# Echelon form for the depthwise filters and seven half groups in parts: an attention and perception kernel on one core

## The chip, the cores and the metric

The kernel runs on one core of a Trainium2 chip. A core has five engines that run their own instruction queues in order: TensorE (PE, matrix products), VectorE (DVE), ScalarE (ACT), GpSimd (POOL) and SyncE (SP, which here only issues DMAs). Products land in PSUM banks of 128 x 512 fp32; everything else lives in SBUF, on 128 partitions. The metric is the device time of the whole kernel in microseconds, from one launch, as the median of several runs.

## The reference

The input is four images of 64 x 64 pixels with 256 channels. Layer 0 is full self attention over the 4096 pixels of an image, with 32 channels for queries and keys. Layer 1 is a depthwise 3x3 convolution with three filters to a channel, two pointwise layers with a GELU between them, and attention over the 3x3 neighbourhood. Cut to what matters here:

```
# layer 0
q, k, v = x @ Wq + bq, x @ Wk + bk, x @ Wv + bv
attn = softmax(q @ k.T)                       # 4096 x 4096 for each image
x = gamma * (attn @ v) + x
# layer 1
perceived = conv(x, w_perc, groups=256) + b_perc      # 768 maps, three filters of 9 taps to a channel
hid = gelu(w_up1 @ perceived + b_up1)                 # 512 x 768
h = x + w_up2 @ hid + b_up2
out = h + local_attention_3x3(h)
```

The pointwise layer after the convolution is linear in the three maps of a channel. So any invertible mix of a channel's three filters, with the inverse mix applied to the three columns of w_up1, gives the same result.

## The kernel before

The 4 x 4096 pixels are cut into 32 slots of 512 queries, eight to an image. A slot goes over the 4096 keys of its image in 16 half groups h = 0 to 15 of 256 keys; the code calls them points and writes h as 2 * G + half. At each point the code issues, in this order:

- the keys and values of the groups ahead, through SP's queue (load_keys, load_values, load_forms);
- high_part of the next half group, where that one is done in parts (ACT);
- energy two half groups ahead: two products into the one buffer e, and exp from e to a tile p on ACT (three buffers);
- jobs[point]: pieces of layer 1 for slots three and five back (hidden_part, update, guide, local_values, scores, local_product), mostly TensorE and VectorE;
- product of this half group: p times the values, added up in the acc banks;
- add_up of the next half group on DVE: the running sum den of the weights p, for the softmax's denominator;
- some steps of the depthwise convolution (perceive) of the slot two back, as many as the list share gives for this point.

An ordinary half group multiplies fp32 p and fp32 values: four products, each of which is two instructions in the trace (acc L402, x8). A half group **in parts** (IN_PARTS, and in_two_sums for the slot) uses fp32r operands instead: p is split into a high part (ACT, tile ph, L388), a low part (DVE, pl, L433) and a combination of both (DVE, gap, tile pg, L434), the values likewise when they are made (vh, vl, vg, L346 to L351, written to memory as packed_f). Three sets of four products (acc L414, x12) then stand for the four fp32 ones. ph, pl and pg have one buffer each. Before, h = 2, 5, 8, 11 and 14 are done so, in 29 of the 32 slots: slots 0, 2 and 31 have none.

perceive makes the six maps of 128 channels (three filters in each half of the channels) of a slot. Tap 0 is an ACT instruction (L587), taps 1 to 8 are one DVE scalar_tensor_tensor each (L591, 128 x 526): 48 in a slot. Twelve cheaper additions (L597) then prepare a fast product of 2 x 2 blocks, whose weights GpSimd makes once from w_up1 (mix_weights, L635). The list mixed holds these 60 steps in order; in the last two slots the lists upper, lower and whole do without the fast product. Slot 31 is the last of the main loop, and a tail outside the loop finishes layer 1.

When the last product of a slot is issued, partial_sums turns and reduces den on DVE, TensorE folds the result (dps, L476), and finish scales acc and adds it to the input (DVE, L479 to L500). In the slots before a new image (7, 15, 23) and in slot 0, the values and keys of blocks to come are projected too (project_v, project_qk). In slot 0, w_perc is loaded at point 8 through GpSimd's queue; w_up1 follows in slot 1 at point 2 and mix_weights in slot 1 at point 8. Watched sums check the result's range, and a slower second version, shifted, would run only if they overflow.

Of the kernel before, what the change touches and what calls it, by code (L numbers as in the profile page):

```python
# [9 lines left out]
F32 = mybir.dt.float32  # L10
F32R = mybir.dt.float32r
AF = mybir.ActivationFunctionType
ALU = mybir.AluOpType
# [3 lines left out]
P = 128  # L17
B, H, W, C = 4, 64, 64, 256
N = H * W
CQK = C // 8  # L20
CH = C // P
HP, WP = H + 2, W + 2
NB = 512
# [5 lines left out]
TAPS = 9  # L29
# [4 lines left out]
MULT = 3  # L34
NPC = MULT * CH
# [4 lines left out]
NG = NT // GRP  # L40
# [8 lines left out]

SPLIT = 4096.0  # L50
BELOW = 1.0 - 2.0**-13
IN_PARTS = (2, 5, 8, 11, 14)


LAG_PERC, LAG_HID, LAG_ATT = 2, 3, 5
# [3 lines left out]
def attention_then_perception_kernel(  # L59
# [19 lines left out]
    nc = tc.nc  # L79

    const = ctx.enter_context(tc.tile_pool(name="const", bufs=1))

    def loaded(src, name, shape=None, queue=None):
        t = const.tile(list(shape or src.shape), F32, tag=name, name=name)
        (queue or nc.sync).dma_start(out=t, in_=src)
        return t
# [10 lines left out]
    def unshifted():  # L97
        fctx = ExitStack()
        pool = fctx.enter_context(tc.tile_pool(name="fast", bufs=1))
# [4 lines left out]
        def tile_of(shape, tag, name, bufs=1):  # L104
            return pool.tile(shape, F32, tag=tag, name=name, bufs=bufs)
# [57 lines left out]
        for r in range(KR):  # L163
            m = near[r * KW : (r + 1) * KW]
            for half in range(2):

                for sign in (1, -1):
                    nc.gpsimd.affine_select(
                        out=m[:, half], in_=m[:, half], compare_op=ALU.is_ge, fill=0.0,
# [13 lines left out]
        for q in range(0, P, SQ):  # L183
            part = fold[q : q + SQ].rearrange("p (j r) -> p j r", r=SQ)
            nc.gpsimd.affine_select(
                out=part, in_=part, compare_op=ALU.not_equal, fill=1.0,
# [29 lines left out]
        def in_parts(s, G, half):  # L216
            return in_two_sums(s) and 2 * G + half in IN_PARTS

# [149 lines left out]
        weights, highs, lows, gaps = {}, {}, {}, {}  # L368
        sums, accs, lsums, lrdens = {}, {}, {}, {}
# [51 lines left out]
        def add_up(s, G, half):  # L421

            p = weights[s, G, half]
            if G == 0 and half == 0:
                sums[s] = tile_of([P, 2, NB], "den", f"den_{s}")
                nc.vector.tensor_copy(sums[s], p)
                return
            den = sums[s]
            nc.vector.tensor_tensor(den, den, p, ALU.add)  # L429
            if in_parts(s, G, half):  # L430
                high = highs[s, G, half]
                low, gap = (tile_of([P, 2, NB], f"p{n}", f"p{n}_{s}_{G}_{half}") for n in "lg")
                nc.vector.tensor_tensor(low.bitcast(F32R), p, high, ALU.subtract)  # L433
                nc.vector.scalar_tensor_tensor(  # L434
                    gap.bitcast(F32R), low, -SPLIT, high, ALU.mult, ALU.add
                )
                lows[s, G, half], gaps[s, G, half] = low, gap
            if G == NG - 1 and half == 1:
                nc.vector.tensor_tensor(den[:, 0, :], den[:, 0, :], den[:, 1, :], ALU.add)
# [163 lines left out]
                    begin(i)  # L603

        def by_turns(outputs, taps, r0, r1):
            return [(i, tap, r0, r1) for tap in taps for i in outputs]

# [18 lines left out]
        lower = by_turns(range(NPC), range(LOW, TAPS), RB - 1, RB)  # L626


        wmix = pool.tile([P, 3, MULT, C], F32, tag="wmix", name="wmix")

        def mix_weights(y11, y12, y21, y22, t1, t2, t4):
            for to, a, b in ((t1, y12, y11), (t2, y22, t1), (t4, y21, t2), (y12, y22, y12)):
                nc.gpsimd.tensor_tensor(to, a, b, ALU.subtract)  # L635

        def blocks_of(w, kin, n):

# [441 lines left out]
        for slot in range(NSLOT):  # L1080
            b, g = divmod(slot, NBLK)
# [20 lines left out]
            if slot == 0:  # L1102
                nxt = [early_jobs[2 * i : 2 * i + 2] for i in range(NG)]
            conv = perceive(slot - LAG_PERC, mixed) if slot >= LAG_PERC else iter(())
            n_mixed = NPC * (TAPS - 1) + MULT * len(MIXED)
            n_steps, stepped = n_mixed, 0


            share = [2, 5, 7, 6, 3, 4, 9, 3, 6, 7, 3, 3, 1, 1, 0, 0]
            if slot == NSLOT - 1:  # L1110

                jobs = [
                    job(hidden_part, k, 0, 0) + job(local_values, k - 1, 1),
                    job(local_denominator, a) + job(hidden_part, k, 0, 1),
                    job(hidden_part, k, 1, 0), job(hidden_part, k, 1, 1) + job(local_product, a, 0),
                    job(update, k, 0), job(update, k, 1) + job(local_product, a, 1),
                    job(guide, k, 0) + job(local_values, k, 0),
                    job(guide, k, 1) + job(local_values, k, 1),  # L1120
                    job(scores, k, 0) + job(hidden_part, k + 1, 0, 0),
                    job(scores, k, 1) + job(local_sum, k - 1) + job(hidden_part, k + 1, 0, 1),
                    job(hidden_part, k + 1, 1, 0) + job(local_total, a + 1)
                    + job(local_reciprocal, a + 1),
                    job(hidden_part, k + 1, 1, 1), job(update, k + 1, 0) + job(border, k),
                    job(local_product, a + 1, 0) + job(update, k + 1, 1),
                    job(local_product, a + 1, 1) + job(local_values, k + 1, 0),
                    job(local_values, k + 1, 1),
                ]
                conv = chain(conv, perceive(slot - 1, upper))  # L1130
                n_steps += NPC * (TAPS - 1)
            for point in range(points):
                G, half = divmod(point, 2)
                after = slot + (G + 1) // NG, (G + 1) % NG
                if half == 0:
                    ahead = slot + (G + 2) // NG, (G + 2) % NG
                    if ahead[0] < NSLOT:
                        load_keys(*ahead)
                    if 0 < ahead[0] < NSLOT:
                        load_values(*ahead)  # L1140
                    if G == NG // 2 and slot + 1 < NSLOT:
                        spread_queries(slot + 1)
                behind = slot + (point + 1) // points, *divmod((point + 1) % points, 2)
                if in_parts(*behind):
                    high_part(*behind)
                if after[0] < NSLOT:
                    energy(*after, half)
                soon = slot + (point + 3) // points, *divmod((point + 3) % points, 2)
                if in_parts(*soon):
                    load_forms(*soon)  # L1150
                for do in jobs[point]:
                    do()
                if slot == NSLOT - 1 and point == NHC + 2 * RING:
                    nc.sync.dma_start(out=wup1[:, :MULT, C:], in_=w_up1[:, :MULT, C:])
                product(slot, G, half)

                if point == 0:
                    add_up(slot, 0, 0)
                if point < points - 1:
                    add_up(slot, *divmod(point + 1, 2))  # L1160
                else:
                    partial_sums(slot)


                if slot < NSLOT - 1:
                    to = sum(share[: point + 1])
                else:
                    to = min(n_steps, -(-(point + 1) * n_steps // (points - 2)))
                    if point < 3:
                        to = min(to, n_mixed // MULT)  # L1170
                while stepped < to:
                    next(conv, None)
                    stepped += 1
                if slot == 0 and point == NG:

                    next(combine)
                    blqk = loaded(b_lqk, "blqk", queue=nc.gpsimd)
                    wperc = loaded(w_perc, "wperc", queue=nc.gpsimd)
                    bperc = loaded(b_perc, "bperc", queue=nc.gpsimd)
                if slot == 1 and point == 2:  # L1180
                    wup1 = loaded(w_up1, "wup1", queue=nc.gpsimd)
                    bup1 = loaded(b_up1, "bup1", queue=nc.gpsimd)
                if slot == 1 and point == NG:
                    wup2 = loaded(w_up2, "wup2", queue=nc.gpsimd)
                    mix_weights(
                        *blocks_of(wup1, MULT, C), *(wmix[:, i] for i in range(3))
                    )
                    bup2 = loaded(b_up2, "bup2", queue=nc.gpsimd)
                    nc.gpsimd.dma_start(out=wlv, in_=w_qkv[:, :, 2 * C :])
                    blv = loaded(b_lv.partition_broadcast(P), "blv", [P, C], queue=nc.gpsimd)  # L1190
                if nxt and half == 1:
                    for do in nxt[G]:
                        do()
                    if slot and G + 2 < NBLK:
                        fetch(slot + 1 + G + 2)
# [470 lines left out]
```

## Time and profile before

| what | value |
|---|---|
| median of 3 runs | 3325.75 us (3325.44 to 3326.32) |
| profiled execution, whole | 3326.11 us |
| its span, first to last instruction | 3323.9 us |
| granted TensorE clock | 0.998 |
| acc L402, direct products | 2936 instructions, 8 to a half group |
| acc L414, products in parts | 3 kinds of 580, 12 to a half group |
| perception taps L591 | 1554 instructions, 1099.6 us |
| sums den L429 | 480 instructions, 602.8 us |
| first copy of a sum, L426 | 32 instructions, 21.9 us |
| DMA | 374.77 MB, 112 GB/s over the span |

In the profile a line names the engine, the operation, the tile it writes and the tiles it reads, then busy time and mean time of one. "Idle before" is how long the engine stood still before such instructions and what ended that. The chain of waits starts from the last instruction and goes back each time to whatever released it, so it lists the work that in fact set the end. Instructions on one engine overlap a little, so the distance from one start to the next is shorter than the duration shown.

### The profile page before, as it was taken

How to read it: one execution, taken by the hardware profiler on the slowest of the kernel's cores; microseconds unless marked ns; L12 is line 12 of the kernel's file. 1: busy time of each engine (PE TensorE's matmuls, PEld its weight loads, DVE VectorE, ACT ScalarE, POOL GpSimd, SP SyncE). 2: the span in 40 equal slices, each digit the busy share in tenths (PEclk: the TensorE clock that was granted, in tenths of full speed). 3: DMA queues.
4: the chain of work that ended last, by engine and by line, in shares of the span. 5: the costliest groups of instructions: out<-in, count | busy, mean ns of one | idle time of the engine just before them, and what ended most of it. 6: DMA issues, size and time to landing. Idle time of an engine off the chain costs nothing.

```text
span 3323.9 us, 34616 instructions
## 1 busy us (share of the span) xinstructions
PE 3298.4 (99%) x11754; PEld 2126.2 (64%) x11754; DVE 2903.3 (87%) x4248; ACT 1276.9 (38%) x1577; POOL 426.4 (13%) x602
## 2 busy tenths in 40 slices
PE   9999999999999999999999999999999999999998
PEld 5556666666666666676666666666666666666655
DVE  3689999878999999987999999997799999999995
ACT  4334433344343333334333433334433434333331
POOL 2200011110111110111001111101110011111021
PEclk9999999999999999999999999999999999999999
DMA  6533333463333333346333333335533333333100
GB/s 189 179 104 105 98 102 103 123 187 124 99 108 108 108 115 97 102 140 196 93 108 98 108 108 108 116 97 159 174 121 92 104 103 108 108 108 108 54 18 27
DMA packets 228743, 374.77 MB, mean 113 GB/s; under 512 B 90080, under 2 KB 91120, under 8 KB 228432
## 3 DMA queue, kind: packets, MB, share of 16 engines
q1 hardware_dynamic: 214928, 339.73, 34.0%
q0 software_dynamic: 5376, 18.26, 1.5%
q10 hardware_dynamic: 8256, 14.49, 1.2%
q8 instruction: 97, 1.59, 0.2%
q14 instruction: 86, 0.70, 0.1%
HBM read 316.51 MB, written 55.05 MB: 112 GB/s over the span
## 4 chain that ended last, share of the span: by engine, by line
PE 96%; DVE 2%; ACT 1%; SPq 0%; issue 0%; DMA 0%; ACTq 0%; DVEq 0%; POOL 0%
PE acc L402 37%; PE acc L414 12%; PE e L378 7%; PE dx L718 6%; PE hid_bc L661 5%; PE hid_gf L661 5%; PE hid_de L661 5%; PE lv L881 3%; PE g L814 3%; PE v L325 3%; PE lo L1015 3%; PE s L922 3%; PE hid_a L661 2%; DVE perc L591 1%; PE qk L259 1%; PE hid L693 1%
## 5 line engine op out<-in xcount | busy, mean ns | idle before, releaser
L402 PE MATMUL acc<-p,v 128*128 128x512 f32 x2936 | 1320.7, 592 | 0.2 <-ACT v L339 0.2
L591 DVE SCALAR_TENSOR_TENSOR perc<-xp,wperc,perc 128x526 f32<-128x526 f32 (+3 forms) x1554 | 1099.6, 773 | 6.8 <-ACT perc L587 6.7
L383 ACT ACTIVATE p<-e 128x1024 f32<-128x1024 f32 x512 | 524.7, 1025 | 1414.0 <-PE e L378 1334.9
L402 PEld LDWEIGHTS acc<-p,v 128*128 128x128 f32 x2936 | 554.0, 190 | 584.1 <-issue 568.5
L429 DVE TENSOR_TENSOR den<-den,p 128x1024 f32<-128x1024 f32 x480 | 602.8, 1256 | 32.2 <-ACT p L383 30.3
L378 PE MATMUL e<-qa,ka 128*128 128x512 f32 x1024 | 450.8, 521 | 5.7 <-ACT p L383 5.7
L947 POOL TENSOR_TENSOR lp<-lp,near 128x396 f32<-128x396 f32 x60 | 79.4, 1323 | 2050.1 <-ACT lp L942 2050.0
L378 PEld LDWEIGHTS e<-qa,ka 128*128 128x128 f32 x1024 | 190.0, 189 | 180.1 <-issue 155.4
L718 PE MATMUL dx<-hid,wup 128*128 128x512 f32 x512 | 229.8, 592 | 0.0
L414 PE MATMUL acc<-ph,v 128*128 128x512 f32 x580 | 184.7, 440 | 0.0
L434 DVE SCALAR_TENSOR_TENSOR pg<-pl,ph 128x1024 fp32r<-128x1024 f32 x145 | 178.1, 1229 | 7.4
L597 DVE TENSOR_TENSOR perc<-perc 128x262 f32<-128x262 f32 x360 | 178.3, 509 | 6.3
L433 DVE TENSOR_TENSOR pl<-p,ph 128x1024 fp32r<-128x1024 f32 x145 | 183.6, 1266 | 0.0
L970 POOL TENSOR_TENSOR lsum<-lsum,lp 128x99 f32<-128x99 f32 (+1 forms) x179 | 170.6, 960 | 11.7
L684 ACT ACTIVATE hid<-hid,bup 128x512 f32<-128x512 f32 x120 | 80.1, 715 | 216.6 <-DVE hid L668 216.6
L718 PEld LDWEIGHTS dx<-hid,wup 128*128 128x128 f32 x512 | 96.6, 189 | 98.3 <-issue 92.9
L414 PE MATMUL acc<-pg,vf 128*128 128x512 f32 x580 | 158.9, 395 | 0.1
L414 PE MATMUL acc<-pl,vf 128*128 128x512 f32 x580 | 157.6, 393 | 0.0
L388 ACT ACTIVATE ph<-p 128x1024 fp32r<-128x1024 f32 x145 | 152.4, 1051 | 0.2
L587 ACT ACTIVATE perc<-xp,bperc,wperc 128x526 f32<-128x526 f32 (+1 forms) x192 | 147.6, 819 | 1.8 <-DVE xp L500 1.8
L414 PEld LDWEIGHTS acc<-pg,vf 128*128 128x128 f32 x580 | 109.0, 188 | 26.5 <-DVE pg L434 0.9
L414 PEld LDWEIGHTS acc<-pl,vf 128*128 128x128 f32 x580 | 109.5, 189 | 25.4 <-DVE pl L433 0.3
(187 smaller groups left out, 3756.7 us busy)
## 6 DMA issues: line engine op xcount, KB each, us to landing
vf<-packed_f SPq DMA_DIRECT2D x145, 512.0 KB, 4.6
ka<-packed SPq DMA_DIRECT2D x1016, 64.0 KB, 1.9
v<-packed_v SPq DMA_DIRECT2D x103, 512.0 KB, 3.7
v<-packed_f SPq DMA_DIRECT2D x145, 256.0 KB, 2.8
v<-packed_v SPq DMA_DIRECT2D x145, 256.0 KB, 2.9
xp<-in_x SPq DMA_DIRECT2D x30, 528.0 KB, 6.7
xc<-in_x SPq DMA_DIRECT2D x56, 256.0 KB, 4.3
out<-lo SPq DMA_DIRECT2D x56, 256.0 KB, 2.1
```

The costliest lines, as they stand in the source:

```text
L378: nc.tensor.matmul(e[:, i, :], lhsT=keys[s, G][:, bass.ts(2 * half + i, P)].bitcast(F32R), rhs=queries[s].bitcast(F32R), start=True, stop= ...
L383: nc.scalar.activation(p, e, AF.Exp)
L402: nc.tensor.matmul(accs[s][c], lhsT=v[:, i, bass.ts(c, P)], rhs=p[:, i, :], start=(first and i == 0), stop=(last and i == 1),)
L414: nc.tensor.matmul(accs[s][to + c], lhsT=w[:, i, bass.ts(c, P)].bitcast(F32R), rhs=x[:, i, :].bitcast(F32R), start=(to > 0 and n == 0 and ...
L429: nc.vector.tensor_tensor(den, den, p, ALU.add)
L433: nc.vector.tensor_tensor(low.bitcast(F32R), p, high, ALU.subtract)
L434: nc.vector.scalar_tensor_tensor(gap.bitcast(F32R), low, -SPLIT, high, ALU.mult, ALU.add)
L591: nc.vector.scalar_tensor_tensor(acc, win, wt, acc, ALU.mult, ALU.add)
L597: nc.vector.tensor_tensor(t[:, to, :], t[:, a, :], t[:, b, :], op)
L661: nc.tensor.matmul(ps[:, n * C : (n + 1) * C], lhsT=w(j), rhs=rows_of(mixes[s, j][:, kind, :]), start=(j == 0), stop=(j == MULT - 1),)
L718: nc.tensor.matmul(ps, lhsT=wup2[:, d, bass.ts(c, P)], rhs=hids[s][:, d, :], start=(d == 0), stop=(d == NHC - 1),)
L970: nc.gpsimd.tensor_tensor(to, to, near_ws[block, half][:, t_, of, :], ALU.add)
```

## The change

The change does five things.

1. IN_PARTS becomes 2, 4, 6, 8, 10, 12, 14: every second half group from 2 on is done in parts in the 29 slots, and the values of those half groups are split when they are made.
2. The three filters of a channel are brought to echelon form in slot 0, at points 5, 6 and 7 (clear_tap, 20 small DVE instructions each): a row exchange by size, then a subtraction that makes one tap zero. Filter 1 loses tap 8, filter 2 loses taps 7 and 8. At points 9 to 14 the matching columns of w_up1 are turned back (turn_weights, four DVE instructions of 128 x 512 each time).
3. by_turns leaves the zero taps out: 42 DVE taps to a slot instead of 48, and 54 steps instead of 60; share is written anew for 54 steps.
4. add_up makes the low part ahead of the sum, and the first sum of a slot is one addition of two tiles, without the copy.
5. w_perc, b_perc and w_up1 are loaded in slot 0 at point 1, and a quarter of the turned w_up1, which mix_weights overwrites, is kept in memory (turned_up) and read back near the end instead of the original.

```diff
-IN_PARTS = (2, 5, 8, 11, 14)
+IN_PARTS = (2, 4, 6, 8, 10, 12, 14)
...
                 sums[s] = tile_of([P, 2, NB], "den", f"den_{s}")
-                nc.vector.tensor_copy(sums[s], p)
                 return
-            den = sums[s]
-            nc.vector.tensor_tensor(den, den, p, ALU.add)
             if in_parts(s, G, half):
                 high = highs[s, G, half]
                 low, gap = (tile_of([P, 2, NB], f"p{n}", f"p{n}_{s}_{G}_{half}") for n in "lg")
                 nc.vector.tensor_tensor(low.bitcast(F32R), p, high, ALU.subtract)
+            den = sums[s]
+            before = weights[s, 0, 0] if (G, half) == (0, 1) else den
+            nc.vector.tensor_tensor(den, before, p, ALU.add)
+            if in_parts(s, G, half):
                 nc.vector.scalar_tensor_tensor(
                     gap.bitcast(F32R), low, -SPLIT, high, ALU.mult, ALU.add
                 )
...
-            return [(i, tap, r0, r1) for tap in taps for i in outputs]
+            return [(i, tap, r0, r1) for tap in taps for i in outputs if tap < TAPS - i % MULT]
...
+        coef = pool.tile([P, MULT, 3, CH], F32, tag="coef", name="coef")
+        ROUNDS = ((1, 2, TAPS - 1), (0, 1, TAPS - 1), (1, 2, TAPS - 2))
+
+        def clear_tap(n):
+            p, q, tap = ROUNDS[n]
+            swap, back, m = (coef[:, n, i, :] for i in range(3))
+            a, b = (scratch[:, i, :] for i in range(2))
...
+            def times(to, k, f, op):
+                v.tensor_tensor(prod, f, k.unsqueeze(2).to_broadcast([P, CH, TAPS + 1]), ALU.mult)
+                v.tensor_tensor(to, to, prod, op)
...
+            times(fp, swap, fq, ALU.add)
+            times(fq, back, fp, ALU.add)
+            times(fp, swap, fq, ALU.add)
...
+            times(fq, m, fp, ALU.subtract)
+            v.tensor_tensor(a, y, b, ALU.mult)
+            times(fq, a, fp, ALU.subtract)
+            v.tensor_tensor(m, m, a, ALU.add)
+
+        def turn_weights(n, half):
+            p, q, _ = ROUNDS[n]
+            up, uq = (wup1[:, half * MULT + i, :] for i in (p, q))
+            swap, back, m = (coef[:, n, i, half : half + 1] for i in range(3))
+            for to, k, of in ((uq, back, up), (up, swap, uq), (uq, back, up), (up, m, uq)):
+                nc.vector.scalar_tensor_tensor(to, of, k, to, ALU.mult, ALU.add)
...
-            share = [2, 5, 7, 6, 3, 4, 9, 3, 6, 7, 3, 3, 1, 1, 0, 0]
+            share = [2, 4, 8, 6, 4, 1, 7, 3, 6, 3, 4, 2, 2, 1, 1, 0]
...
-                    nc.sync.dma_start(out=wup1[:, :MULT, C:], in_=w_up1[:, :MULT, C:])
+                    nc.sync.dma_start(out=wup1[:, :MULT, C:], in_=turned_up)
...
+                if slot == 0 and point == 1:
+                    wb = const.tile([P, CH, MULT, TAPS + 1], F32, tag="wb", name="wb")
+                    nc.gpsimd.dma_start(out=wb[:, :, :, :TAPS], in_=w_perc)
+                    bias = loaded(b_perc, "bperc", queue=nc.gpsimd)
+                    wperc, bperc = wb[:, :, :, :TAPS], wb[:, :, :, TAPS]
+                    wup1 = loaded(w_up1, "wup1", queue=nc.gpsimd)
+                    bup1 = loaded(b_up1, "bup1", queue=nc.gpsimd)
+                if slot == 0 and NG - MULT <= point < NG:
+                    if point == NG - MULT:
+                        scratch = tile_of([P, NB], "rden", "scratch")
...
+                        nc.vector.tensor_copy(bperc, bias)
+                    clear_tap(point - NG + MULT)
+                if slot == 0 and NG < point <= NG + 2 * MULT:
+                    turn_weights(*divmod(point - NG - 1, 2))
                 if slot == 0 and point == NG:
...
-                    wperc = loaded(w_perc, "wperc", queue=nc.gpsimd)
-                    bperc = loaded(b_perc, "bperc", queue=nc.gpsimd)
-                if slot == 1 and point == 2:
-                    wup1 = loaded(w_up1, "wup1", queue=nc.gpsimd)
-                    bup1 = loaded(b_up1, "bup1", queue=nc.gpsimd)
                 if slot == 1 and point == NG:
+                    nc.gpsimd.dma_start(out=turned_up, in_=wup1[:, :MULT, C:])
```

More of the change, by code (lines that the diff above doesn't have):

```diff
@@ L626, in unshifted @@
         lower = by_turns(range(NPC), range(LOW, TAPS), RB - 1, RB)
+        turned_up = tc.dram_tile([P, MULT, C], F32, name="turned_up")
         wmix = pool.tile([P, 3, MULT, C], F32, tag="wmix", name="wmix")
@@ L635, in mix_weights @@
                 nc.gpsimd.tensor_tensor(to, a, b, ALU.subtract)
+        coef = pool.tile([P, MULT, 3, CH], F32, tag="coef", name="coef")
[4 more added lines that the diff above has]
+            a, b = (scratch[:, i, :] for i in range(2))
+            prod = scratch[:, 2:, :].rearrange("p j c -> p c j")
+            fp, fq = (wb[:, :, i, :] for i in (p, q))
+            x, y = (wb[:, :, i, tap] for i in (p, q))
+            v = nc.vector
+            def times(to, k, f, op):
+                v.tensor_tensor(prod, f, k.unsqueeze(2).to_broadcast([P, CH, TAPS + 1]), ALU.mult)
+                v.tensor_tensor(to, to, prod, op)
+            v.scalar_tensor_tensor(a, x, -1.0, x, ALU.mult, ALU.max)
+            v.scalar_tensor_tensor(b, y, -1.0, y, ALU.mult, ALU.max)
+            v.tensor_tensor(swap, b, a, ALU.is_gt)
+            v.tensor_scalar(back, swap, -1.0, None, ALU.mult)
+            times(fp, swap, fq, ALU.add)
+            times(fq, back, fp, ALU.add)
+            times(fp, swap, fq, ALU.add)
+            v.tensor_scalar(a, x, 0.0, None, ALU.is_equal)
+            v.tensor_tensor(a, a, x, ALU.add)
+            v.reciprocal(b, a)
+            v.tensor_tensor(m, y, b, ALU.mult)
+            times(fq, m, fp, ALU.subtract)
[8 more added lines that the diff above has]
+                nc.vector.scalar_tensor_tensor(to, of, k, to, ALU.mult, ALU.add)
         def blocks_of(w, kin, n):
@@ L1104, in unshifted @@
             conv = perceive(slot - LAG_PERC, mixed) if slot >= LAG_PERC else iter(())
-            n_mixed = NPC * (TAPS - 1) + MULT * len(MIXED)
+            n_mixed = sum(tap != 0 for _, tap, *_ in mixed)
             n_steps, stepped = n_mixed, 0
-            share = [2, 5, 7, 6, 3, 4, 9, 3, 6, 7, 3, 3, 1, 1, 0, 0]
+            share = [2, 4, 8, 6, 4, 1, 7, 3, 6, 3, 4, 2, 2, 1, 1, 0]
             if slot == NSLOT - 1:
@@ L1130, in unshifted @@
                 conv = chain(conv, perceive(slot - 1, upper))
-                n_steps += NPC * (TAPS - 1)
+                n_steps += sum(tap != 0 for _, tap, *_ in upper)
             for point in range(points):
@@ L1173, in unshifted @@
                     stepped += 1
+                if slot == 0 and point == 1:
[8 more added lines that the diff above has]
+                        scratch = tile_of([P, NB], "rden", "scratch")
+                        scratch = scratch[:, : (TAPS + 3) * CH].rearrange("p (j c) -> p j c", c=CH)
+                        nc.vector.tensor_copy(bperc, bias)
+                    clear_tap(point - NG + MULT)
+                if slot == 0 and NG < point <= NG + 2 * MULT:
+                    turn_weights(*divmod(point - NG - 1, 2))
                 if slot == 0 and point == NG:
```

## The prediction

> **What bounds the kernel now.** I read the engine shares of the page first, then the chain of waits of one ordinary slot, the busy time of that slot by engine, VectorE's own waits in it, and the chain at the end.
>
> The page, parts 1 and 5 (busy us, then mean ns of one):
>
> ```profile
> PE 3298.4 (99%) x11754; PEld 2126.2 (64%) x11754; DVE 2903.3 (87%) x4248; ACT 1276.9 (38%) x1577; POOL 426.4 (13%) x602
> ...
> L591 DVE SCALAR_TENSOR_TENSOR perc<-xp,wperc,perc 128x526 f32<-128x526 f32 (+3 forms) x1554 | 1099.6, 773 | 6.8 <-ACT perc L587 6.7
> ...
> L434 DVE SCALAR_TENSOR_TENSOR pg<-pl,ph 128x1024 fp32r<-128x1024 f32 x145 | 178.1, 1229 | 7.4
> ...
> L433 DVE TENSOR_TENSOR pl<-p,ph 128x1024 fp32r<-128x1024 f32 x145 | 183.6, 1266 | 0.0
> ```
>
> TensorE has no idle time worth the name; VectorE has 421 us in all. The chain in an ordinary slot (start us, us, what):
>
> ```profile
> 896.16 1.54 PE lo L1015 x12
> 897.70 2.81 PE acc L414 x12
> ...
> 911.72 3.43 PE acc L402 x8
> 915.16 0.46 PE e L378 x2
> 915.62 1.72 PE g L814 x4
> 917.34 2.77 PE acc L414 x12
> ...
> 945.52 0.13 PE c L865 x2
> 945.65 2.99 PE acc L414 x12
> ```
>
> Every piece is TensorE's. A half group done directly costs 3.43 us, one in parts 2.77 us, or 2.81 behind lo and 2.99 behind the tiny border product c. That difference is the prize. One ordinary slot (us; busy time by engine, clock, DMA share, GB/s), and what VectorE waited for in it:
>
> ```profile
> 888.77:986.10 97.33, 97.33 (x349) 63.50 (x348) 90.51 (x131) 38.21 (x47) 11.55 (x13) 1.00 0.34 106
> ```
>
> ```profile
> DVE hid L668 <- PE hid_gf L661: 2.2, 2, 1.4
> DVE inverse L479 <- PE dps L476: 1.4, 1, 1.4
> DVE hid L668 <- PE hid_de L661: 1.4, 1, 1.4
> ```
>
> TensorE is busy for all 97.33 us, VectorE for 90.51, and VectorE's gaps are waits on TensorE. So a shorter TensorE stream shortens the kernel, as long as VectorE, with under 7 us in hand per slot, keeps up. The one stretch where VectorE carries the chain is after the last slot:
>
> ```profile
> 3210.32 3.52 DVE perc L591 x18
> ...
> 3216.54 11.97 DVE perc L591 x15
> ```
>
> [...] a direct product is 3.43/4 = 0.86 us, a part 2.77/12 = 0.23. [...] while GpSimd mixed weights at 119.7 to 130.9, sums (L429) took 2.8 us instead of 1.2. [...] the sums are 1.22 us.
>
> **The change, part by part.** h is the half group 0 to 15 of a slot.
>
> *Two more half groups in parts.* In 29 of the 32 slots (not 0, 2, 31) the list goes from h = 2, 5, 8, 11, 14 to 2, 4, 6, 8, 10, 12, 14. TensorE per slot: before, five in parts at 2.77+2.81+2.77+2.77+2.99 = 14.11 and eleven direct, 11 x 3.43 + 0.03 = 37.76; after, seven at 2.77+2.81+4 x 2.77+2.99 = 19.65 (h = 4 now stands behind lo) and nine direct, 30.90. That is 50.55 instead of 51.87: -1.32 us a slot, **-38.3 us** in all. It lies on the path.
>
> *What VectorE pays.* 58 more pairs of low and gap at 1.266 + 1.229: +144.7 us. The cleared taps leave three of 27 out per half of the channels: 6 of 48 operations in each slot's perception. In 30 slots 180 x 0.713 (1027.4 us over 1440, by form) = -128.4, in the last two -9.5. The copy of the first sum goes, its add takes both tiles: 32 x 0.683 = -21.9. Eight more value half groups are split (28 for 20; 0.69 + 0.69 + 0.43): +14.5. Clearing adds 60 operations on 2 to 20 elements; the nearest row, the border's 128x8 ones, repeats every 0.2 to 0.26 us when dependent: about +15[...]. Turning the weights is 24 operations at 0.7 to 0.75: +17. Net VectorE is up by some 32 us, all of it in slot 0, where it is 30% busy; an ordinary slot stays at 90.
>
> *Does VectorE keep pace within a slot?* I laid the new VectorE list along the new TensorE list, from dps to dps, with pitches of the trace (tap 0.69, mix step 0.41, sum or part 1.14). Points 0 to 3 still end in waits on hid_de, hid_gf and hid_bc. Then the queue drains without a gap: gap of h = 4 is ready at 35.5 us and TensorE wants it at 38.7; h = 6 48.7 against 50.9; h = 8 61.0 against 63.2; h = 10 70.6 against 73.7; h = 12 80.7 against 83.5; h = 14 88.7 against 91.0. The row sums for dps come at 94.5 to 95.0, TensorE reaches dps at 95.85. So 1 to 3 us in hand everywhere: 0 us in plain slots. In the eight slots at an image's edge VectorE has 1.1 us more (91.5 to 91.6 busy): I take **+1 us** for all, bounds 0 and 9.
>
> *Buffers.* ph, pl and pg have one buffer each. Between two parts now lie two points instead of three. From the start of a part: ph's products 0.9, ACT's high 1.05, then low, sum and gap 3.5, so 5.5 us; the shortest two points (12 and 13) last 4.57 + 3.90 = 8.47. About 3 us in hand, so 0. ScalarE adds 58 x 1.05 = 61 us to 1277. The vf loads grow by 58 x 512 KB = 30 MB on 375; DMA stands at 0.34 in this slot, loads are asked for three points ahead and land in 4.6 us: 0. SP and its queue have the same order, and waited for the products of the point before already.
>
> *Slot 0.* The weights load moves from slot 1 to point 1: 1.5 MB at about 30 to 42 us, among the start's loads, and GpSimd's queue is free there (last issue before it at 29.35). ka for point 4 is issued at 40.67 and used at 46.44: bounds 0 and 4, I take +0.5. The first sum now waits for p of h = 1 where a copy of 0.61 us stood on the chain at 33.17: +0.5. Clearing needs some 5 us at points 5, 6, 7, where VectorE idles 6.7, 7.6 and 8.3 us before its next input; turning 2.9 us at points 9 to 13: hidden. The last turning stands at point 14, ahead of partial_sums: row sums were ready at 108.7 for a dps at 109.5, now at about 111.4: **+1.9 us** on the path.
>
> *Start of slot 1.* GpSimd's mixing no longer waits for the load (it began at 119.7) but follows the row sums, at about 113.5[...]. By hand: sum of h = 1 at about 123, so exp of h = 3 and then e of h = 4 are some 4 us late; before, e of h = 7 came 3.2 us late at 133.15 and the part behind it took 4.35 instead of 2.77. Net **+0.5**, bounds -3 and +5. turned_up (384 KB out, back in at the end) has time at both ends: 0.
>
> *The three slots that project the next image.* One or two more splits each in VectorE's queue, which waits up to 8 us for ScalarE's vh: +1, bounds 0 and 6.
>
> *End.* 18 small taps become 12: 6 x 0.2 = **-1.2**. The 32 taps before the next update stay 32; the six saved there come later, beside TensorE.
>
> Sum: -38.3 + 1 + 0.5 + 0.5 + 1.9 + 0.5 + 1 - 1.2 = -34.1. The profiled run took 3326.11 us for a span of 3323.9, and the median shown is 3325.75; from 3325.75 that is **3291.5 us** (span about 3290).
>
> **Rivals.** *VectorE bounds the slots.* Its last wait in a slot, before dps, falls from 1.4 us to below 1; for it speak the 90 of 96 us, against it the laid-out list. If the list is 1 us too short, 29 slots x 0.5 to 1 us give back 15 to 29: 3306 to 3320.
>
> *Slower: the single ph, pl and pg become the bound.* If the chain part, high, low, gap doesn't fit between two parts because ScalarE's high stands behind an exp or VectorE's low behind taps, every part makes TensorE wait, 29 x 7 = 203 times. The gain is eaten from 34.1/203 = 0.17 us per part on; at 0.3 it is 3291.5 + 61 = 3352. For it: exp waited on pl seven times before, up to 7.3 us, with the next part two points further off. Against: of those waits only the one in slot 1 reached TensorE (its own waits for exp are 5.7 us in the whole run), and the hand list leaves over 2 us.
>
> *Half the gain.* The turned weights or their start cost what I bounded from above (4 + 5 + 6 + 1.9): 3304, inside my range. *The reduced taps are not what runs:* then VectorE has 138 us more, 4.1 a slot, and no slack to hold it: about 98 us a slot, slower than before; the steps are cut in the same list that is issued, so I give it nearly nothing.
>
> **How the numbers follow.** My case 0.76, VectorE bound 0.14, single buffers 0.06, half the gain 0.03, unreduced taps 0.01. The unknown costs of my case span -5 (slot 1 and start at their lower ends) to +17, and a part priced 0.05 us too high or too low adds 58 x 0.05 = 3 to either side; the first rival reaches 3320. Leaving out a tenth on each side gives 3282 to 3311. A change of 0.2% is 6.7 us, about what can be told from none. Faster: 0.76 + 0.11 + 0.03 = 0.90 (a quarter of the first rival could lose more than its 1 us a slot); same 0.03; slower 0.06 + 0.01.
>
> **What would show it.** acc L414 should count 812 of each kind, at 2.8 us a dozen, acc L402 2472 (309 half groups); an ordinary slot should last 96.0 us with VectorE near 90 busy and the wait before dps under 1 us. If the chain shows DVE partial sums or pg pieces in ordinary slots, VectorE or the single buffers decide. Around 107 to 135 us the chain should show the turning and the mixing. I am wrong if parts behind dx or lv cost 3 us and not 2.77, or if slots last over 96.5.

## The result, and the profile after

The changed kernel takes 3306.45 us (median of 4 runs, 3304.45 to 3307.91) against 3326.03 us before on the same chip (3325.44 to 3326.35): a ratio of 0.9941, with a 95% interval of 0.9924 to 0.9958. The profiled run took 3305.77 us for a span of 3304.1, before 3326.11 for 3323.9. So 19.6 us were gained where the sum said 34.1; the time lies inside the range of the prediction, 3282 to 3311.

The page of the changed kernel, parts 1 and 5 (busy us, mean ns of one, idle before and what ended it):

```profile
PE 3264.6 (99%) x11986; PEld 2170.4 (66%) x11986; DVE 2905.2 (88%) x4243; ACT 1349.2 (41%) x1647; POOL 500.7 (15%) x627
...
L592 DVE SCALAR_TENSOR_TENSOR perc<-xp,wb,perc 128x526 f32<-128x526 f32 (+1 forms) x1356 | 969.1, 773 | 0.1
...
L378 PE MATMUL e<-qa,ka 128*128 128x512 f32 x1024 | 427.9, 499 | 13.0 <-ACT p L383 13.0
...
L388 ACT ACTIVATE ph<-p 128x1024 fp32r<-128x1024 f32 x203 | 214.4, 1056 | 199.4 <-PE acc L414 130.5
L414 PE MATMUL acc<-ph,v 128*128 128x512 f32 x812 | 264.4, 447 | 0.0
L430 DVE TENSOR_TENSOR pl<-p,ph 128x1024 fp32r<-128x1024 f32 x203 | 253.2, 1247 | 12.1 <-ACT ph L388 12.0
```

VectorE's busy time is what it was (2905.2 us against 2903.3): 198 taps went, 58 pairs of low and gap came. TensorE's busy time fell by 33.8 us, the span by 19.8, so some 14 us of it now stand as waits; the wait of e for ScalarE's p alone is 13.0 us, against 5.7 before. The busy time of four stretches, each from one slot's dps to the next, shows where (us, then busy time of PE, PEld, DVE, ACT, POOL, clock, DMA share, GB/s): slot 0, slot 1, slot 14 and slot 23.

```profile
0.00:120.34 120.34, 105.97 (x344) 61.44 (x345) 63.78 (x135) 43.21 (x61) 25.70 (x72) 0.97 0.62 198
120.34:183.29 62.95, 61.30 (x198) 37.81 (x199) 45.40 (x43) 24.80 (x25) 12.80 (x12) 0.97 0.56 171
...
1337.24:1433.29 96.05, 96.05 (x358) 64.98 (x357) 89.78 (x127) 40.53 (x48) 13.24 (x13) 1.00 0.39 117
...
2240.47:2375.47 135.00, 132.19 (x517) 90.70 (x516) 103.33 (x149) 59.16 (x81) 19.90 (x31) 1.00 0.59 188
```

In the ordinary slot TensorE is busy for all of 96.05 us, as forecast. Slot 23 contains 2.8 us, and slot 0 over 14 us, in which it isn't. Slot 0 before, in the same columns:

```profile
0.00:109.35 109.35, 104.15 (x344) 60.70 (x345) 34.73 (x45) 41.19 (x57) 21.54 (x65) 1.00 0.61 187
```

| stretch | forecast, us | measured, us |
|---|---|---|
| slot 0, to its dps | +0.5 +0.5 +1.9 = +2.9 | 109.35 to 120.34 = +11.0 |
| slot 1 | -1.32 + 0.5 = -0.8 | 65.69 to 62.95 = -2.7 |
| slots 3 to 30 | 28 x -1.32 + 1 + 1 = -35.0 | 2832.37 to 2802.13 = -30.2 |
| last dps to last computation | -1.2 | 107.8 to 107.6 = -0.2 |
| last computation to end of span | 0 | 8.5 to 11.0 = +2.4 |
| slots 2 and 31 | 0 | 0.0 |
| sum | -34.1 | -19.8 |

The chain of waits through slot 0 of the changed kernel (start us, us, what):

```profile
26.76 2.68 SPq L85
29.44 0.04 issue
29.48 9.74 DMA gbv<-in_b_v
...
39.31 0.23 DVE gbv L1110
...
39.60 1.14 DVE den L433
...
40.82 1.03 ACT p L383
...
41.90 1.22 PE e L378 x2
43.12 4.54 PE acc L402 x8
```

gbv is a bias of 1 KB. VectorE multiplies it by gamma, and the next sum of weights stands behind that in its queue. The same place before:

```profile
29.30 3.50 DMA gbv<-in_b_v
...
35.67 3.43 PE acc L402 x8
```

The load was on the chain before, and took 3.50 us. Now it takes 9.74, so the first product after this gap starts 7.45 us later and takes 1.1 us longer: over it and the e ahead of it (41.90 to 47.66 us) the granted clock was 0.71, before 1.00. The end of slot 0 in the same chain:

```profile
115.83 0.67 DVE wup L679
116.53 0.76 DVE wup L679
117.31 0.76 DVE wup L679
118.10 0.75 DVE wup L679
118.85 0.63 DVE turned L458
119.51 0.69 DVE parts L459
...
120.34 0.59 PE dps L477 x2
```

Here the last turning of w_up1 (wup) stands ahead of the row sums (turned, parts), and TensorE waits 2.2 us for them. What VectorE itself waited for in the ordinary slot, 14 (us in total, times, longest; hid_de, hid_gf and hid_bc are products of the hidden layer):

```profile
DVE hid L712 <- PE hid_de L705: 2.1, 1, 2.1
DVE hid L712 <- PE hid_gf L705: 1.4, 1, 1.4
DVE hid L712 <- PE hid_bc L705: 1.0, 1, 1.0
DVE inverse L480 <- PE dps L477: 0.8, 1, 0.8
```

The last line is 1.4 before. It is not all time in hand, since a part of it is the way to dps and back. In slot 0, where TensorE waited for VectorE, dps starts 0.14 us after the row sums end; in an ordinary slot VectorE goes on 0.34 us after dps starts. That leaves, as an estimate, 1.38 - 0.48 = 0.9 us in hand before the change (slot 14) and 0.76 - 0.48 = 0.3 us after it.

### The profile page after: what moved, and what is told of

Same layout as the page of the kernel before. It is cut to its first block, busy times and chain, and to the rows that moved or that the text cites. A ratio compares the mean times of both kernels' runs of the same rounds, so it can differ in the third digit from the quotient of the medians.

```text
span 3304.1 us, 35658 instructions
## 1 busy us (share of the span) xinstructions
PE 3264.6 (99%) x11986; PEld 2170.4 (66%) x11986; DVE 2905.2 (88%) x4243; ACT 1349.2 (41%) x1647; POOL 500.7 (15%) x627
## 4 chain that ended last, share of the span: by engine, by line
PE 92%; DVE 4%; DMA 1%; ACT 1%; issue 1%; SPq 0%; POOL 0%; ACTq 0%; DVEq 0%; POOLq 0%
PE acc L402 30%; PE acc L414 16%; PE e L378 7%; PE dx L762 6%; PE hid_bc L705 5%; PE hid_gf L705 5%; PE hid_de L705 5%; PE lv L925 3%; PE g L858 3%; PE v L325 3%; PE lo L1059 3%; PE s L966 2%; PE hid_a L705 2%; DVE perc L592 2%; PE qk L259 1%; PE hid L737 1%
## 5 line engine op out<-in xcount | busy, mean ns | idle before, releaser
L402 PE MATMUL acc<-p,v 128*128 128x512 f32 x2472 | 1113.5, 593 | 0.2 <-ACT v L339 0.2
L592 DVE SCALAR_TENSOR_TENSOR perc<-xp,wb,perc 128x526 f32<-128x526 f32 (+1 forms) x1356 | 969.1, 773 | 0.1
L402 PEld LDWEIGHTS acc<-p,v 128*128 128x128 f32 x2472 | 466.8, 190 | 486.8 <-issue 472.5
L991 POOL TENSOR_TENSOR lp<-lp,near 128x396 f32<-128x396 f32 x60 | 150.8, 2513 | 1965.3 <-ACT lp L986 1965.3
L388 ACT ACTIVATE ph<-p 128x1024 fp32r<-128x1024 f32 x203 | 214.4, 1056 | 199.4 <-PE acc L414 130.5
L414 PE MATMUL acc<-ph,v 128*128 128x512 f32 x812 | 264.4, 447 | 0.0
L430 DVE TENSOR_TENSOR pl<-p,ph 128x1024 fp32r<-128x1024 f32 x203 | 253.2, 1247 | 12.1 <-ACT ph L388 12.0
L435 DVE SCALAR_TENSOR_TENSOR pg<-pl,ph 128x1024 fp32r<-128x1024 f32 x203 | 256.7, 1264 | 0.0
L414 PE MATMUL acc<-pg,vf 128*128 128x512 f32 x812 | 222.0, 395 | 1.1 <-DVE pg L435 1.1
L414 PE MATMUL acc<-pl,vf 128*128 128x512 f32 x812 | 219.6, 392 | 0.0
L414 PEld LDWEIGHTS acc<-ph,v 128*128 128x128 f32 x812 | 148.3, 189 | 51.0 <-issue 26.8
L414 PEld LDWEIGHTS acc<-pg,vf 128*128 128x128 f32 x812 | 152.5, 188 | 37.0 <-DVE pg L435 1.5
L414 PEld LDWEIGHTS acc<-pl,vf 128*128 128x128 f32 x812 | 152.7, 188 | 35.6 <-DVE pl L430 0.4
```

Of the source, the lines that this page charges most:

```text
L388: nc.scalar.activation(high.bitcast(F32R), weights[s, G, half], AF.Identity, scale=BELOW)
L402: nc.tensor.matmul(accs[s][c], lhsT=v[:, i, bass.ts(c, P)], rhs=p[:, i, :], start=(first and i == 0), stop=(last and i == 1),)
L414: nc.tensor.matmul(accs[s][to + c], lhsT=w[:, i, bass.ts(c, P)].bitcast(F32R), rhs=x[:, i, :].bitcast(F32R), start=(to > 0 and n == 0 and ...
L435: nc.vector.scalar_tensor_tensor(gap.bitcast(F32R), low, -SPLIT, high, ALU.mult, ALU.add)
L592: nc.vector.scalar_tensor_tensor(acc, win, wt, acc, ALU.mult, ALU.add)
```

## The experiments

Each run but those that say otherwise is the changed kernel with one edit. Ratios are against the kernel before on the same chip.

**The weights load.** In the changed kernel GpSimd issues the loads at 27.9 to 30.4 us and then nothing until the stores of the next split values, which wait for ScalarE until 57.4. So only a place behind these stores moves the load of w_up1.

```diff
                     bias = loaded(b_perc, "bperc", queue=nc.gpsimd)
                     wperc, bperc = wb[:, :, :, :TAPS], wb[:, :, :, TAPS]
+                if slot == 0 and point == 4:
                     wup1 = loaded(w_up1, "wup1", queue=nc.gpsimd)
                     bup1 = loaded(b_up1, "bup1", queue=nc.gpsimd)
```

> The load of w_up1 and b_up1 goes from slot 0 point 1 to point 4, where it stands in GpSimd's queue behind the stores of the next split values and so starts at about 60 us; w_perc and b_perc stay at point 1. Theory (the 1.5 MB load delays the tiny load gbv): gbv lands in about 3.5 us after its issue instead of 9.74, the first product after the gap starts near 36 us instead of 43.1, slot 0 ends 7 to 8.5 us earlier, the run takes about 3298.5. Rival (the small pieces of w_perc and b_perc are what delays it): gbv still takes 8 to 10 us and the time stays at 3306.

Measured: 3299.6 us, ratio 0.9919 (0.9902 to 0.9936). Its chain:

```profile
29.75 4.05 DMA gbv<-in_b_v
...
36.48 0.97 PE e L378 x2
37.45 4.87 PE acc L402 x8
```

gbv lands in 4.05 us although w_perc and b_perc still go out at point 1, so it is the 1.5 MB that delays it, and slot 0 falls to 114.98 us. That is 5.4 us and not the 7 to 8.5 expected, because the first product starts at 37.45 and not near 36 us, and still runs slowly (4.87 us). GpSimd issues its load and SyncE the bias, on separate queues, and gbv still took 9.74 us with the load issued 0.2 us ahead of it and 4.05 without; how one holds up the other is not shown. Two more kernels with the load at point 1, gbv behind it and seven parts agree: in all_taps and late_sums the e behind this wait starts at 41.83 and 41.87 us, in the changed kernel at 41.90 and in late_weights at 36.48.

**The other end of the same wait.** The loads of gamma and gbv are put ahead of the input blocks 4 and 5:

```diff
+        gam = loaded(gamma.partition_broadcast(P), "gam", [P, 1])
+        gbv = loaded(b_v.rearrange("o (c p) -> p (o c)", p=P), "gbv")
         fetch(4)
         fetch(5)
-        gam = loaded(gamma.partition_broadcast(P), "gam", [P, 1])
-        gbv = loaded(b_v.rearrange("o (c p) -> p (o c)", p=P), "gbv")
```

> gamma and gbv are loaded ahead of the input blocks 4 and 5 instead of behind them; the weights load stays at point 1. Theory (VectorE's first sum waits only for gbv): VectorE has gbv by about 28 us, the first product after the gap starts near 34.5 us instead of 43.1, with a full clock it takes 3.43 instead of 4.54, slot 0 loses 9 to 10 us of its 120.3, the run takes about 3297. Rival (it is the traffic of the load that holds the start, not this one wait): another load, the input blocks or the keys for point 4, becomes the wait in the same place and less than 4 us are gained, 3302 or more.

Measured: 3303.31 us, ratio 0.9933 (0.9916 to 0.9949); the rival is right. VectorE has gbv at 26.4 us, but the chain only changes its load, and slot 0 still takes 118.43 us:

```profile
26.56 11.62 DMA xc<-in_x
...
38.23 1.97 PE qk L259 x2
40.19 1.15 PE e L378 x2
```

An input block takes 11.6 us beside the weights, and TensorE waits 4.36 us for it (0.27 in front_taps below, where they are out of the way). So it is the traffic that costs: take away the wait for one load, and another one takes its place.

**The turnings of w_up1.** They go from points 9 to 14 to points 7 to 12:

```diff
-                if slot == 0 and NG < point <= NG + 2 * MULT:
-                    turn_weights(*divmod(point - NG - 1, 2))
+                if slot == 0 and NG <= point + 1 < NG + 2 * MULT:
+                    turn_weights(*divmod(point - NG + 1, 2))
```

> The six turnings of w_up1 stand at points 7 to 12 of slot 0 instead of 9 to 14. Theory: the last one no longer stands between the last sum and the row sums, TensorE's wait of 2.2 us before dps in slot 0 goes to 0, nothing else changes, 3304.2. Rival (VectorE's queue is full from point 9 on, so it only moves the lateness to a sum): the wait stays or turns up before a product, 3306.

Measured: 3303.29 us, ratio 0.9931 (0.9915 to 0.9948). The wait of 2.16 us before dps is gone, and slot 0 goes from 120.34 to 118.09 us, -2.25. The runs of these kernels spread over 2.5 to 7 us, and with the same start slot 0 took 120.3 to 122.4 us from one kernel's trace to another's. So it is the wait that shows the gain, and not the medians.

**Slot 23.** ScalarE writes projected queries and keys into tiles st, which here share four buffers with the split values. In the changed kernel the second st tile waits there for the store of a split value, and TensorE's e waits 2.81 us for the exp behind it (start us, us, what, idle before):

```profile
2366.37 0.69 ACT L271 ACTIVATE st<-qk,bqk 128x512 f32<-128x512 f32 x1 [3.39 <-DMA packed_f<-vh]
```

```diff
-                tag, bufs = ("o", 2) if s < NBLK else ("vs", 4)
+                tag, bufs = ("o", 2)
```

> The tiles st of the projected queries and keys use the two buffers of o in every slot, as they do for the first image, instead of the four buffers shared with the split values. Theory (in slot 23 the second st tile waits for the store of a split value, since a half group that is split and also kept whole takes four of these four buffers): the wait of 2.8 us before e in slot 23 goes, slot 23 takes about 132.1 instead of 135.0, slots 7 and 15 stay at 132.0, the run 3303.5. Rival (ScalarE is late there because of VectorE and GpSimd's sum): slot 23 stays at 135, 3306.

Measured: 3304.07 us, ratio 0.9934 (0.9917 to 0.9950). The slot has no wait on TensorE any more:

```profile
2242.26:2374.20 131.94, 131.94 (x517) 90.78 (x516) 103.22 (x149) 58.52 (x81) 22.06 (x31) 1.00 0.60 193
```

That is 3.06 us less than the 135.00 above. In the other kernels with the shared buffers and seven parts the slot took 134.1 to 136.1 us, so the gain is 2.2 us at the least. Slots 7 and 15 take 131.9, beside 132.0 in the changed kernel. The rest of the run drowns in the start's spread: slot 0 took 122.4 us in this run.

**The two halves of the change.** First the parts without the echelon form; the filters keep their 27 taps, and w_up1 is not turned:

```diff
-            return [(i, tap, r0, r1) for tap in taps for i in outputs if tap < TAPS - i % MULT]
+            return [(i, tap, r0, r1) for tap in taps for i in outputs]
...
-            share = [2, 4, 8, 6, 4, 1, 7, 3, 6, 3, 4, 2, 2, 1, 1, 0]
+            share = [2, 5, 7, 6, 3, 4, 9, 3, 6, 7, 3, 3, 1, 1, 0, 0]
...
-                    clear_tap(point - NG + MULT)
-                if slot == 0 and NG < point <= NG + 2 * MULT:
-                    turn_weights(*divmod(point - NG - 1, 2))
```

> Seven half groups in parts, but all 48 taps: the filters are not brought to echelon form and w_up1 is not turned; share is the old one, the loads stay as after the change. VectorE has 6 x 0.69 = 4.1 us more a slot. Theory (VectorE is level with TensorE: in the plain slot that was read the row sums end 0.42 us before dps starts, and its waits of 4.5 us at points 0 to 3 can't be filled because its order is fixed): a plain slot takes 99.6 to 100 us instead of 96.05, the run about 3405 to 3415, slower than before. Rival, as in the prediction (about 1 us in hand before dps, and part of the early waits filled): about 98 us a slot, 3355 to 3365.

Measured: 3393.93 us, ratio 1.0204 (1.0187 to 1.0221), between the totals that theory and rival named. A plain slot (13), and what TensorE waits for in it:

```profile
1271.58:1371.01 99.43, 97.00 (x357) 64.61 (x357) 93.48 (x133) 40.66 (x48) 12.03 (x14) 1.00 0.37 114
```

```profile
PE acc L414 <- DVE pg L435: 2.4, 3, 1.1
```

VectorE is busy for 93.48 us and TensorE is no longer full: it waits for pg, the last tile of a part. 3.7 us more of VectorE's busy time cost 3.4 us a slot (96.07 to 99.43), a little less than the theory's 3.6 to 4 and well over the rival's 2. With the share of before and the loads at point 1, parts alone make the kernel 2% slower; leaving out the six taps pays for them. Whether another share would have saved some of it was not tried.

Then the echelon form without the new parts:

```diff
-IN_PARTS = (2, 4, 6, 8, 10, 12, 14)
+IN_PARTS = (2, 5, 8, 11, 14)
```

> Echelon form, turned weights, new loads and new share, but the half groups in parts are 2, 5, 8, 11, 14 as before. Theory (TensorE sets the slot, and the gain is that of two dozens of products in parts): a plain slot is back at 97.3 us although VectorE has some 2.5 x 2 = 5 us less in it, slot 0 stays near 120, slot 23 near 133, the run takes about 3342, slower than before by the start. Rival (the lighter VectorE alone shortens the slots): below 97.0 us a slot and below 3330.

Measured: 3328.27 us, ratio 1.0007 (1.0001 to 1.0014). An ordinary slot:

```profile
1345.58:1442.90 97.32, 97.32 (x350) 63.51 (x348) 85.44 (x123) 38.18 (x46) 11.33 (x13) 1.00 0.35 106
```

Slot 14 above and the other slots are what the theory said: TensorE takes 97.32 us although VectorE fell to 85.44, and slots 3 to 30 sum to 2831.64 us against 2832.37 before. So the lighter VectorE alone is worth 0.7 us there, and the new parts 29.5. The total of 3342 was wrong: it added the forecast's 38 instead of the 30 that the slots show, and kept slot 0 at 120 where it took 114.9. The second has a reason in GpSimd's queue. With h = 4 in parts the stores of block 2 come from its first pair of values, with h = 5 from its second, some 2 us later. What follows in the queue, first of the changed kernel:

```profile
27.36 0.54 POOL L353 DMA_DIRECT2D packed_f<-vg  x1
27.89 0.85 POOL L1220 DMA_DIRECT2D wb<-in_w_perc  x1
28.73 0.55 POOL L85 DMA_DIRECT2D bperc<-in_b_perc  x1
29.28 0.53 POOL L85 DMA_DIRECT2D wup<-in_w_up  x1
```

and of this run:

```profile
29.22 0.54 POOL L353 DMA_DIRECT2D packed_f<-vg  x1
...
31.14 0.53 POOL L85 DMA_DIRECT2D wup<-in_w_up  x1
```

SyncE issues gbv at 29.48 and at 28.88 us. So in the changed kernel the big load goes out just ahead of gbv, and here 2.3 us behind it: gbv is off the chain, and a load of keys (5.52 us) stands in its place.

**VectorE's time in hand.** The turning of the row sums (a transpose) is done twice in slots 3 to 30, which is extra work and nothing else:

```diff
-                nc.vector.transpose(turneds[s][:, i, :], t)
+                for _ in range(2 if 3 <= s < NSLOT - 1 and i == 0 else 1):
+                    nc.vector.transpose(turneds[s][:, i, :], t)
```

> In slots 3 to 30 the turning of the row sums before dps (0.70 us on VectorE) is done twice, with the same result. Theory (VectorE has at most 0.42 us in hand before dps in plain slots and none at an image's edge): plain slots 96.4 to 96.75, edge slots 97.2 to 97.4, the run 10 to 18 us longer, 3317 to 3325. Rival, as the prediction laid it out (1 us in hand): plain slots stay at 96.05, the run below 3312.

Measured: 3320.34 us, ratio 0.9981 (0.9975 to 0.9988). A plain slot (13) and one at an image's edge (11):

```profile
1246.11:1342.58 96.47, 96.33 (x357) 64.91 (x357) 90.50 (x128) 40.55 (x48) 13.52 (x14) 1.00 0.38 118
```

```profile
1052.13:1149.57 97.44, 96.41 (x357) 64.91 (x357) 91.32 (x132) 40.46 (x48) 15.91 (x19) 1.00 0.38 117
```

They were 96.07 and 96.71. Of the extra 0.70 us, 0.4 to 0.5 reach most plain slots and all of it an edge slot: VectorE had 0.2 to 0.3 us in hand in the one, as estimated above, and none in the other.

**The places together.** late_weights, gbv_first, turn_early and st_other_buffer in one kernel:

> The changed kernel with w_up1 loaded at point 4, gamma and gbv loaded ahead of blocks 4 and 5, the turnings at points 7 to 12, and st in the buffers of o. Theory (the four places are separate waits; with w_up1 out of the way blocks 4 and 5 land in time): 5.4 for the late load, 2.2 for the turnings, 2.9 in slot 23 and 2 to 4 for gbv, 3291 to 3294. Rival (the start has a further wait behind these, the input blocks themselves): gbv early adds nothing or costs, 3295 to 3298.

Measured: 3292.58 us, ratio 0.9900 (0.9883 to 0.9916). Slot 0 takes 110.44 us, 9.9 less than in the changed kernel, and its first product runs in 3.43 us again. The four places add up: what the first three gained alone in slot 0 (5.4, 1.9 and 2.3 us) comes to 9.5. An input block is still on the chain there.

**Work for VectorE's early waits.** The last step starts from all_four and moves three taps, one each from points 8, 9 and 10, to point 0, behind which VectorE stands idle for hid_de:

```diff
-            share = [2, 4, 8, 6, 4, 1, 7, 3, 6, 3, 4, 2, 2, 1, 1, 0]
+            share = [5, 4, 8, 6, 4, 1, 7, 3, 5, 2, 3, 2, 2, 1, 1, 0]
```

> all_four with three taps of the convolution moved to point 0 of each slot (share begins 5, 4, 8 instead of 2, 4, 8; points 8 and 9 give two of them, point 9 and 11 none else changes: 5, 2, 3, 2 there). Theory (VectorE is late before dps because it stands idle 2.1 us at point 1 for hid_de; work put there comes back as time in hand at the end): the wait at hid_de goes to about 0, the six slots at an image's edge fall from 96.5 and 96.7 to their TensorE time, 96.3 and 96.4, plain slots stay at 96.05, the run gains 1 to 2 us, 3290.5 to 3291.5. Rival (the taps delay lrden and the next hid, and with it the hidden layer on TensorE): TensorE waits at hid or c at points 1 to 4 and slots last over 96.3, 3295 or more.

Measured: 3288.18 us (3287.85 to 3288.37), ratio 0.9887 (0.9871 to 0.9904), the fastest of all. VectorE's waits in a plain slot (13):

```profile
DVE inverse L480 <- PE dps L477: 2.1, 1, 2.1
DVE hid L712 <- PE hid_gf L705: 1.7, 2, 1.4
DVE hid L712 <- PE hid_bc L705: 1.0, 1, 1.0
...
```

The 2.1 us for hid_de are gone, and the wait before dps has grown from 0.8 to 2.1. Edge slots take 96.12 and 96.14 us, now as much as TensorE is busy, and less than the 96.3 and 96.4 expected: so part of what counted there as TensorE's busy time was delay. Slots 3 to 30 gave 3.4 us, more than the 1 to 2 expected. Slots 0 and 1 were 1.0 us shorter too, but no taps run in them, so that is not the edit's. The same kernel with the doubled turning:

> front_taps with the turning of the row sums done twice in slots 3 to 30, as in late_sums. Theory (the taps at point 0 give VectorE some 2 us in hand before dps): the extra 0.70 us costs nothing, plain slots 96.05 and edge slots 96.4 or less. Rival (VectorE's work before dps is held by the last p, not by its own queue): plain slots again 96.5 and edge slots over 97.

Measured: 3289.13 us in one run; plain slots 96.05 to 96.07 and edge slots 96.11 to 96.14. The 0.70 us that cost 0.4 to 0.7 us a slot in late_sums cost nothing here.

## Why the prediction was right or wrong

**Right: what bounds, and what the parts are worth.** TensorE's stream sets the ordinary slot. old_parts and the changed kernel differ by 1.27 us in most slots, beside a forecast of 1.32: the seven parts of a slot, twelve products each, last 19.70 us and not 19.65, which over nineteen slots makes +1.0. The counts came as written (812 of each kind of L414, 2472 direct), and the parts behind dx and lv took 2.77 to 2.79 us. In no plain slot does TensorE wait for ph, pl or pg, so the rival of the single buffers fell. It is ScalarE that now waits for the one ph until TensorE has read it, 130.5 us in the run where it was 0.2 before, and that doesn't reach TensorE. When VectorE is late, as in all_taps, TensorE does wait for its pg, 75 times and 65 us in the run; whether the single buffers add to that isn't shown. (From 3325.75 the sum of -34.1 gives 3291.65, not 3291.5.)

**Nearly wrong: VectorE keeps pace.** The 0 us for plain slots held, but by less than the prediction said. The hand list had row sums at 94.5 to 95.0 us for a dps at 95.85, so about 1 us in hand; late_sums measures 0.2 to 0.3. Its sign, a wait before dps of under 1 us, was met with 0.76 us, of which some 0.5 is the way there and back. VectorE's work was summed rightly by busy time: the busy times of its groups of instructions add up to 31 us more (3067.9 against 3037.2), beside a forecast of 32, though that of the whole engine, where every overlap counts once, rose by 1.9 alone, and counts times mean durations give 7. For edge slots it took +1 us in all: six of its eight gained 0.90 instead of 1.32, which is +2.5. And where it priced the loss of the reduced taps at "about 98 us a slot", all_taps took 99.4 to 99.7.

**Wrong: the weights load, +0.5 us with bounds 0 and 4.** That is the largest error of the sum: 7.45 us of later start and 1.1 of slow clock, less 0.5 for the sum in place of the copy, so some +8. Its working compared the load with ka for point 4 and saw 6 us of room. It never asked which small load was on the chain while the 1.5 MB flowed, though the profile of before had gbv there with 3.50 us. late_weights takes back 5.4 of it, and all_four leaves 1.1 us of slot 0's 11.0. This is the total of the case "half the gain", 3304 us, but not by its terms: the load went beyond its bound of 4, while slot 1 and the projecting slots stayed below theirs of 5 and 6. At 0.03 costs at the start had far too small a chance, since the bounds for the load rested on one transfer. That the time still lay inside the range is in part luck: its upper end left 17 us for unknown costs, of which this load was to take 4 at most.

**The other terms of the start.** The last turning was priced at +1.9 and cost 2.2 (turn_early: 2.25). Slot 1 gained 2.7 where +0.5 was set against -1.32. In old_parts, with the parts of before, it gains 1.65 of them (65.69 to 64.04), from the load and the mixing in another order; which of the two was not tried apart. The trace shows that e's wait for ScalarE in this slot fell from 3.2 to 0.6 us, and that one of 1.1 us for pg came.

**The projecting slots.** For three of them +1 us was taken for VectorE's queue. Slots 7 and 15 lost 0.1 to 0.2 us each; slot 23 lost 2.9 alone, from the buffers shared by split values and st, which the prediction didn't look at. st_other_buffer shows it.

**The end.** The 18 small taps of 3.52 us fell to 12 of 2.35, but the stretch shrank by 0.2 us and not by 1.2: instructions behind them took longer and gaps of some 0.4 and 0.6 us came. Why is not shown. From the last computation to the end of the span there are 2.4 us more. With the old parts it is 0.8 more, and all kernels with seven parts have about 11. In that stretch SyncE waits for TensorE's queue (3.9 us before, 6.8 in the changed kernel); what holds that longer stays open.

## What to carry to other kernels

A big load that is moved into a busy start is priced by what the chain is waiting for at that time, be it a transfer of 1 KB (3.50 us before, 9.74 in the changed kernel); its own bytes and its own deadline, which had 6 us of room here, don't tell. Where a queue has no waiting instruction, a later line of code need not make a later load: look at the queue's timeline first. Time in hand is a wait less its own round trip, and it is measured by adding work: here by doing a cheap instruction in front of the wait twice. When the engine off the chain is level with the one on it, look for its own idle time early in the loop before cutting its work: three taps moved to point 0 gave VectorE over a microsecond at the end of each slot.

## What the runs showed of the hardware

A 1 KB load (gbv) took 3.50 us in the kernel before and 4.05 in late_weights. In the changed kernel, where a 1.5 MB load had been issued 0.2 us before it from another engine, it took 9.74. An input block took 11.6 us beside that load (gbv_first).

The first direct product after an idle stretch of TensorE in slot 0 was slow: 4.54 us after 8.0 us of waiting, 5.13 after 2.4 (old_parts), and 3.43 after 0.8 in the kernel before; in late_weights it took 4.87. In the changed kernel the granted clock was 1.00 just ahead of the wait (31.93 to 33.88 us), 0.50 from 38.50 to 45.20, of which TensorE works from 41.90 on, and 1.00 from 45.25. Behind the wait of 2.16 us before dps it was 0.50 from 120.34 to 123.34 us, 0.81 in the next microsecond and then 1.00. Behind the wait of 2.81 us in slot 23 it stayed at 1.00 (2368.02 to 2374.00), and in the kernel before, behind 0.8 us, too (34.94 to 39.10).

An estimate from the first of these: 3.3 us of work at half the clock lose 1.65 us. From the start of the e ahead of it to the end of the product, the changed kernel, late_weights and old_parts lost 1.6 to 1.7 us against the kernel before. But all_taps and late_sums, after waits of 7.8 and 7.9 us, lost 2.0 and 2.3. So the estimate has the right size but is no upper bound. What makes the difference, and which waits lower the clock, isn't shown.
